# Layer 0 of a two-layer image network: turning a tile by VectorE blocks and DRAM instead of TensorE, adding the bias on TensorE, subtracting maxima on GpSimd

## The chip, the cores and the metric

The kernel runs on one core of a Trainium2 chip. The core has four computing engines that follow their own instruction streams: TensorE (PE; weight loads are shown apart as PEld), VectorE (DVE), ScalarE (ACT) and GpSimd (POOL). SyncE (SP) issues nearly all transfers between DRAM and on-chip memory (SBUF); TensorE's results arrive in PSUM. The metric is the time on the device in microseconds. The kernel before takes 9257.28 us (median of 3 runs, 9252.85 to 9259.84).

## The reference

The input is 8 images of 128x128 points with 128 channels. Two layers follow each other. Layer 0 is a linear attention, and is the only one that the change touches (N = 128x128, NH = 4 heads of HD = 32):

```python
qkv = einsum('bhwc,cf->bhwf', x, w_qkv); q, k, v = split(qkv, 3)
q, k, v = (t.reshape(B, NH, HD, N) for t in (q, k, v))      # a plain reshape of the memory
q = softmax(q, axis=-2) * HD**-0.5
k = softmax(k, axis=-1)
context = einsum('bhdn,bhen->bhde', k, v)
attn = einsum('bhde,bhdn->bhen', context, q).reshape(B, H, W, 128)
out = einsum('bhwf,fc->bhwc', attn, w_out) + b_out
out = (out - mean(out)) * rsqrt(var(out) + 1e-3) * gamma + beta   # over the channels
x = out + x
```

Layer 1 is a selective scan over each image in four directions: a projection to 512 columns, a 3x3 depthwise convolution, the scans, a gate `silu(z)` on their sum, a layer norm and an output projection. Its gate z is a product of layer 0's output, and the kernel computes it at the end of layer 0.

## The kernel before, in words

The program has three stages one after the other: `layer0`, `layer1_front` and `layer1_scan`. The change lies in `layer0` alone.

`layer0` holds two images in SBUF (`xs`), channels in the partitions and points (w, h) along the free side. An image is worked in NG = 32 groups of GW = 4 columns w, 512 points each. `image(b)` runs two things at once: `attend(b)`, which computes the output of image b, and `context(b + 1)`, which computes the context of the next image from its keys and values. Image -1 has only a context, image 7 (the last) only an attention. The plain reshape of the reference makes each image row h one of its 128 rows (head and d) and puts w and channel along n, so the softmax of k runs along w and channels of one h, and a maximum is needed for each of the 128 h before the exponential. `context` keeps it per section of BK = 4 groups and rescales the sum (`total`) when a new section begins.

The stages of `context` for group g: `key` (matmul, copy to SBUF on ACT), `larger` (running maximum of four groups on VectorE; after the fourth it is cut down to 128 columns in two steps, L196 and L197), `fold` (TensorE turns the maximum, VectorE reduces it to a column m, compares it with the earlier one, forms the exponent a of the rescaling and a diagonal matrix dg), `spread` (a matmul of ones with dg puts the maxima along the free side, in the PSUM tile pm), `subtract` (k minus pm, VectorE L231), `raise_to` (exp on ACT), `value` (matmul, copy on ACT) and `add` (four pairs of matmuls into pc, and once per section total on VectorE).

The stages of `attend`: `query` (matmul into pq, maximum qm L270 and subtraction L272 on VectorE), `exponent` (ACT L275), `normalize` (sum L280 and reciprocal L281 on VectorE, product L282 on GpSimd), `through_wo` (matmuls into pg, copy gt on ACT), `through_context` (matmul into po; VectorE adds the bias, L296, which moves the tile to SBUF as o; ACT squares it, L298), `variance` (VectorE sums the squares, L302), `scale` (GpSimd: var, rstd by a power, L310, and a diagonal matrix d of rstd for each column, L313), `turn` (TensorE multiplies o by d, L321: up to here h is in the partitions and w and channel along the free side; this scales the tile and turns it so that channels are in the partitions again) and `finish` (ACT applies gamma and beta, L325; GpSimd adds x, L327; for half of the images the result is stored, L330). The weights `wo` and the bias `bb` have their means taken off beforehand, so out is already centred.

The order of work is written out by hand. `in_order` makes each engine (SP too) run its instructions in the order in which the program emits them. `image` has one loop over t; in step t each stage works on group t minus its own lag, and contexts lag one step more (`later`, a = t - later). So an instruction that waits holds back all that follows on its engine. The list of `at(...)` calls in `image` is this order.

`gate_group` computes the gate z of layer 1: for some images VectorE first copies the group with w and h exchanged (L152), then two matmuls, two Silu on ACT and two stores. `gate(b - 1)` does this for a whole image after step 0 of image b and then loads image b + 1. In the last image the gates of images 6 and 7 are done inside the steps, two groups per step. Silu and exp each make ACT load their table (ACT_TABLE_LOAD) when they alternate.

PSUM tiles of `layer0` share six slots (`ps`), taken in turn.

Of the kernel before, what the change touches and what calls it, by code (L numbers as in the profile page):

```python
# [8 lines left out]
F32 = mybir.dt.float32  # L9
# [23 lines left out]
NCH = L // CH  # L33
EPS0 = 1e-3
EPS1 = 1e-5


NAT, TURN = 0, 1
# [39 lines left out]
def layer0(ctx: ExitStack, tc, xT, w_qkv, w_out, b_out, gamma, beta, win, x1, zs):  # L78
# [15 lines left out]
    sm = ctx.enter_context(tc.tile_pool(name="l0s", bufs=4))  # L94
    ps = ctx.enter_context(tc.tile_pool(name="l0p", bufs=6, space=PSUM))
    psc = ctx.enter_context(tc.tile_pool(name="l0pc", bufs=1, space=PSUM))

    ident = const.tile([P, P], F32, name="ident")
    make_identity(nc, ident)
# [8 lines left out]
    nc.sync.dma_start(wz, win[:, NC2 * P :])  # L108
    wo = const.tile([P, P], F32, name="wo")
    nc.sync.dma_start(wo, w_out)  # L110
    bb = const.tile([P, GW, P], F32, name="bb")
    for i in range(GW):
        nc.sync.dma_start(bb[:, i, :], b_out.to_broadcast([P, P]))
    gb = const.tile([P, 2], F32, name="gb")
    nc.sync.dma_start(gb[:, 0:1], gamma)
    nc.sync.dma_start(gb[:, 1:2], beta)

    mean = const.tile([P, 2], F32, name="mean")
    nc.vector.tensor_reduce(mean[:, 0:1], wo, AX.X, ALU.add)
    nc.vector.tensor_reduce(mean[:, 1:2], bb[:, 0, :], AX.X, ALU.add)  # L120
    nc.vector.tensor_scalar(mean, mean, 1.0 / P, None, ALU.mult)
    nc.vector.tensor_scalar(wo, wo, mean[:, 0:1], None, ALU.subtract)
    nc.vector.tensor_scalar(bb, bb, mean[:, 1:2], None, ALU.subtract)

    xs = [const.tile([P, W, H], F32, name=f"x{i}") for i in range(2)]
    vts, ctxs = [], []
# [46 lines left out]

    def context(b):

        ks, pks, ms, runs, scales = {}, {}, {}, {}, {}

        def key(g):
            pk = ps.tile([P, GW, P], F32, name="pk", tag="ps")
            nc.tensor.matmul(pk, wq[:, P : 2 * P], group(b, g), start=True, stop=True)  # L180
            ks[g] = k = wp.tile([P, GW, P], F32, name="k", tag="k", bufs=7)
            nc.scalar.copy(k, pk)
            pks[g] = pk

        def larger(g):
            pk = pks.pop(g)
            j, i = divmod(g, BK)
            if i == 1:
                runs[j] = run = wp.tile([P, GW, P], F32, name="run")
                nc.vector.tensor_tensor(run, pk, ks[g - 1], ALU.max)  # L190
            elif i > 1:
                nc.vector.tensor_tensor(runs[j], pk, runs[j], ALU.max)

            if i == BK - 1:
                run = runs[j]
                nc.vector.tensor_tensor(run[:, 0:2], run[:, 0:2], run[:, 2:4], ALU.max)  # L196
                nc.vector.tensor_tensor(run[:, 0], run[:, 0], run[:, 1], ALU.max)  # L197

        def fold(g):

            j, i = divmod(g, BK)
            if i < BK - 1:
                return
            run = runs.pop(j)
            turned = ps.tile([P, P], F32, name="pmt", tag="ps")
            nc.tensor.transpose(turned, run[:, 0, :], ident)
            ms[j] = m = sm.tile([P, 1], F32, name="m")
            nc.vector.tensor_reduce(m, turned, AX.X, ALU.max)
            if j:
                nc.vector.tensor_tensor(m, m, ms[j - 1], ALU.max)  # L210
                scales[j] = a = sm.tile([P, 1], F32, name="a")
                nc.vector.tensor_tensor(a, ms.pop(j - 1), m, ALU.subtract)
            runs[j] = dg = sm.tile([P, P], F32, name="dg", bufs=2)
            nc.vector.tensor_scalar(dg, ident, m, None, ALU.mult)

        def spread(g):
            j, i = divmod(g, BK)
            if i == BK - 1:
                nc.tensor.matmul(pm[:, j % 2, :], ones, runs.pop(j), start=True, stop=True)
                if j:  # L220
                    nc.scalar.activation(scales[j], scales[j], AF.Exp)

        def value(g):
            pv = ps.tile([P, GW, P], F32, name="pv", tag="ps")
            nc.tensor.matmul(pv, wq[:, 2 * P : 3 * P], group(b, g), start=True, stop=True)
            nc.scalar.copy(vts[g % 3][:, :, 0:P], pv)

        def subtract(g):

            mb = pm[:, g // BK % 2 : g // BK % 2 + 1, :]  # L230
            nc.vector.tensor_tensor(ks[g], ks[g], mb.to_broadcast([P, GW, P]), ALU.subtract)  # L231
# [26 lines left out]

        return key, larger, fold, spread, value, subtract, raise_to, add

    def attend(b):

        cn = ctxs[b % 2]
        qs, gs, os, vs, ys = {}, {}, {}, {}, {}

        def query(g):
            pq = ps.tile([P, GW * NH, HD], F32, name="pq", tag="ps")
# [22 lines left out]
            nc.scalar.copy(gt, pg)  # L290

        def through_context(g):
            po = ps.tile([P, GW, P], F32, name="po", tag="ps")
            nc.tensor.matmul(po, cn, gs.pop(g), start=True, stop=True)
            os[g] = o = wp.tile([P, GW, P], F32, name="o", bufs=3)
            nc.vector.tensor_tensor(o, po, bb, ALU.add)  # L296
            vs[g] = sq = wp.tile([P, GW, P], F32, name="sq")
            nc.scalar.activation(sq, o, AF.Square)  # L298

        def variance(g):  # L300
            var = sm.tile([P, GW], F32, name="var")
            nc.vector.tensor_reduce(var, vs[g], AX.X, ALU.add)  # L302
            vs[g] = var

        def scale(g):

            var = vs[g]
            nc.gpsimd.tensor_scalar(var, var, 1.0 / P, EPS0, ALU.mult, ALU.add)
            rstd = sm.tile([P, GW, 1], F32, name="rstd")
            nc.gpsimd.tensor_tensor(rstd[:, :, 0], var, half, ALU.pow)  # L310
            vs[g] = d = wp.tile([P, GW, P], F32, name="d")
            i3 = ident.rearrange("p (o c) -> p o c", o=1)
            nc.gpsimd.tensor_tensor(  # L313
                d, i3.to_broadcast([P, GW, P]), rstd.to_broadcast([P, GW, P]), ALU.mult
            )

        def turn(g):
            o, d = os.pop(g), vs.pop(g)
            ys[g] = pt = ps.tile([P, GW, P], F32, name="pt", tag="ps")
            for i in range(GW):  # L320
                nc.tensor.matmul(pt[:, i, :], o[:, i, :], d[:, i, :], start=True, stop=True)  # L321

        def finish(g):
            y = wp.tile([P, GW, P], F32, name="x1t")
            nc.scalar.activation(y, ys.pop(g), AF.Identity, bias=gb[:, 1:2], scale=gb[:, 0:1])  # L325
            xg = group(b, g)
            nc.gpsimd.tensor_tensor(xg, y, xg, ALU.add)  # L327
            if g % 2 == 1 and ORDER[b] >= B // 2:
                t = xs[b % 2][:, (g - 1) * GW : (g + 1) * GW, :].rearrange("p w h -> p (w h)")
                nc.sync.dma_start(x1[ORDER[b]][:, (g - 1) * GN : (g + 1) * GN], t)  # L330

        return query, exponent, normalize, through_wo, through_context, variance, scale, turn, finish

    def image(b):

        key = larger = fold = spread = value = subtract = raise_to = add = None
        query = exponent = normalize = through_wo = through_context = None
        variance = scale = turn = finish = None
        later = LATER if b >= 0 else 0
        if b + 1 < B:  # L340
            key, larger, fold, spread, value, subtract, raise_to, add = context(b + 1)
        if b >= 0:
            (query, exponent, normalize, through_wo, through_context, variance, scale, turn,
             finish) = attend(b)

        def at(stage, g):
# [2 lines left out]

        for t in range(later + NG + BK + 2):  # L350
            a = t - later
            at(scale, t - 2)
            at(finish, t - 3)
            at(query, t)
            if b == B - 1 and t < NG:
                gate_group(b - 1, t)
            at(through_wo, t - 1)
            if b == B - 1 and 4 <= t < NG + 4:
                gate_group(b, t - 4)
            at(exponent, t)  # L360
            at(subtract, a - BK - 1)
            at(raise_to, a - BK - 1)
            at(key, a)
            at(normalize, t)
            at(fold, a - 1)
            at(value, a - BK - 1)
            at(larger, a)
            at(through_context, t - 1)
            at(add, a - BK - 2)
            at(turn, t - 2)  # L370
            at(spread, a - 1)
            at(variance, t - 1)
            if t == 0 and 0 < b < B - 1:
                gate(b - 1)
# [895 lines left out]
```

## Time and profile before

| | |
|---|---|
| median of the runs | 9257.28 us |
| the profiled execution | 9261.02 us |
| its span, first to last instruction | 9259.2 us |
| mean granted TensorE clock | 0.796 |
| busy over the span: PE, DVE, ACT, POOL | 68%, 86%, 77%, 79% |
| layer 0: up to | 2388 us |
| reciprocal of total (a context is complete), L252 | 110.0, 337.0, 634.8, 933.5, 1221.7, 1507.7, 1804.2, 2099.0 us |
| gate of a whole image, image 3 | from about 936 to 997 us |
| DMA, 0 to 2300 us | 112 GB/s mean |

The profile is of one execution. A line of a group gives the line of the kernel, the engine, the operation, output and input names with their shapes, the count, busy time, the mean of one in ns, the idle time of the engine just ahead of these instructions and what ended it. A line of the timeline gives start and duration in us. Idle time that is marked `<-ACT sq` ended when ACT's instruction that wrote sq was done.

### The profile page before, as it was taken

To read this page: it belongs to the slowest core of one execution; us is meant where nothing else is said; L and a number is where in the kernel's file an instruction comes from. 1 tells how busy PE (TensorE), PEld (TensorE's weight loads), DVE (VectorE), ACT (ScalarE), POOL (GpSimd) and SP (SyncE) were. 2 spreads that over 40 slices of the span, in tenths; PEclk is the share of its full clock that TensorE was granted. 3 is DMA by queue.
4 is the path that set the end of the run, shared out by engine and by line. 5 is a ranking of instruction groups with operands and counts; after the bars stand their busy time and mean duration, and the time that the engine had idled before them with its cause. 6 is when DMAs were issued, how large, how long until landed. Compare 5 with 4: busy or idle time off the path is not lost. (4 is left out here: it accounts for less than half of the span.)

```text
span 9259.2 us, 91316 instructions
## 1 busy us (share of the span) xinstructions
PE 6337.5 (68%) x24512; PEld 3096.6 (33%) x24512; DVE 7992.0 (86%) x7953; ACT 7099.7 (77%) x8066; POOL 7316.5 (79%) x4684
## 2 busy tenths in 40 slices
PE   8899998988899999999434636446364463643636
PEld 5555555554333333333101304114031140311403
DVE  6667666774699999999799999999999999999996
ACT  5555555657789999999688887887878888888885
POOL 3446444554588988888599899998999989999897
PEclk9999999999999999999655757557575575755857
DMA  1322333123478789888758769587695876957767
GB/s 76 146 84 96 137 121 146 70 109 137 148 242 249 251 246 244 245 246 241 206 154 238 208 185 258 158 230 216 179 260 159 222 225 178 257 165 218 230 174 211
DMA packets 934769, 1750.66 MB, mean 189 GB/s; under 512 B 150228, under 2 KB 376148, under 8 KB 926064
## 3 DMA queue, kind: packets, MB, share of 16 engines
q1 hardware_dynamic: 873328, 1509.92, 49.4%
q0 software_dynamic: 60928, 234.90, 13.8%
q8 instruction: 200, 3.28, 0.1%
q14 instruction: 313, 2.56, 0.1%
HBM read 1052.36 MB, written 692.12 MB: 188 GB/s over the span
## 5 line engine op out<-in xcount | busy, mean ns | idle before, releaser
L951 POOL TENSOR_TENSOR h<-ubt,sp 128x1024 f32<-128x1024 f32 x1024 | 2422.4, 2399 | 348.4 <-ACT mv L1058 124.1
L934 PE MATMUL px<-rows,dtw 128*128 128x512 bf16 x2048 | 953.5, 565 | 2266.2 <-DVE y L1001 1084.5
L534 DVE SCALAR_TENSOR_TENSOR acc<-xb,cw,acc 128x1024 f32<-128x1024 f32 x1024 | 1320.3, 1289 | 133.7 <-ACT xb L502 89.9
L526 POOL TENSOR_TENSOR tap<-tap 128x1024 f32<-128x1024 f32 x512 | 1224.0, 2394 | 243.9 <-ACT tap L524 220.6
L938 ACT ACTIVATE sp<-px 128x1024 f32<-128x1024 f32 x1024 | 1047.3, 1024 | 435.4 <-PE px L934 418.1
L961 DVE TENSOR_TENSOR_SCAN h<-px,h 128x1024 f32<-128x1024 f32 x512 | 1177.3, 2331 | 31.7 <-ACT px L942 15.1
L934 PEld LDWEIGHTS <-dtw 128*128 128x128 bf16 x2048 | 169.1, 110 | 3089.1 <-issue 1022.7
L959 DVE TENSOR_TENSOR_SCAN h<-px,h 128x1024 f32<-128x1024 f32 x512 | 1177.9, 2330 | 21.4 <-POOL h L951 18.8
L1009 POOL TENSOR_TENSOR y<-y,h 128x512 f32<-128x512 f32 x768 | 1159.8, 1559 | 3.8 <-DVE h L982 3.8
L942 ACT ACTIVATE px<-sp,sa 128x1024 f32<-128x1024 f32 x1024 | 1110.4, 1109 | 6.1
L515 PE MATMUL acc<-xi,wt 128*128 128x512 f32 x2048 | 938.3, 601 | 53.7 <-ACT ures L539 53.7
L524 ACT ACTIVATE tap<-xb,cw 128x1024 f32<-128x1024 f32 x768 | 837.3, 1139 | 15.2 <-POOL xb L499 15.1
L282 POOL TENSOR_TENSOR q<-q,qs 128x512 f32<-128x512 f32 x256 | 272.2, 1063 | 695.5 <-DVE qs L281 695.5
L938 ACT ACT_TABLE_LOAD x512 | 656.9, 1283 | 170.0 <-PE px L934 168.0
L942 ACT ACT_TABLE_LOAD x512 | 656.9, 1283 | 9.1
L1074 PEld LDWEIGHTS px<-wg,z 128*128 128x128 f32 x4096 | 575.3, 225 | 114.8 <-issue 109.1
L1074 PE MATMUL px<-wg,z 128*128 128x128 f32 x4096 | 574.7, 308 | 0.0
L967 PE MATMUL pc<-rows,csel 128*128 128x512 bf16 x1024 | 517.5, 586 | 78.2 <-DVE rstd L1062 74.5
L515 PEld LDWEIGHTS acc<-xi,wt 128*128 128x128 f32 x2048 | 375.1, 189 | 574.4 <-issue 411.9
L488 PE MATMUL pxb<-xi,wi 128*128 128x512 f32 x1024 | 496.2, 607 | 2.1 <-ACT xb L497 2.1
L298 ACT ACTIVATE sq<-o 128x512 f32<-128x512 f32 x256 | 161.2, 630 | 421.0 <-DVE o L296 419.8
L1001 DVE TENSOR_TENSOR y<-y,px 128x1024 f32<-128x1024 f32 x384 | 468.6, 1220 | 14.4
(153 smaller groups left out, 15038.8 us busy)
## 6 DMA issues: line engine op xcount, KB each, us to landing
ubt<-ubs SPq DMA_DIRECT2D x1024, 512.0 KB
zs<-z SPq DMA_DIRECT2D x512, 256.0 KB
ubs<-ures SPq DMA_DIRECT2D x256, 512.0 KB
ubs<-turned SPq DMA_DIRECT2D x256, 512.0 KB
z<-zs SPq DMA_DIRECT2D x256, 512.0 KB
y<-gs POOLq DMA_DIRECT2D x128, 1024.0 KB, 10.3
gs<-du POOLq DMA_DIRECT2D x96, 1024.0 KB, 8.6
rows<-xps SPq DMA_DIRECT2D x1536, 60.0 KB
```

Of the source, the lines that this page charges most:

```text
L515: nc.tensor.matmul(acc[:, s, :], wt[:, j, c, :], x, start=(j == 0), stop=(j == len(ON_PE) - 1))
L524: nc.scalar.activation(t, at(n, c, *d), AF.Copy, scale=weight(n, c, *d))
L526: nc.gpsimd.tensor_tensor(sums[n, c], sums[n, c], t, ALU.add)
L534: nc.vector.scalar_tensor_tensor(acc, at(n, c, *d), weight(n, c, *d), acc, ALU.mult, ALU.add)
L934: nc.tensor.matmul(p[:, hf * 512 : hf * 512 + 512], sl.dw[:, c * P : c * P + P], src, start=True, stop=True)
L938: nc.scalar.activation(t, da[n, c], AF.Softplus)
L942: nc.scalar.activation(da[n, c], sp[n, c], AF.Exp, scale=sa[:, sl.s, c : c + 1])
L951: nc.gpsimd.tensor_tensor(h, u, t, ALU.mult)
L959: nc.vector.tensor_tensor_scan(e[:, ::-1], x[:, ::-1], e[:, ::-1], start, ALU.mult, ALU.add)
L961: nc.vector.tensor_tensor_scan(e, x, e, start, ALU.mult, ALU.add)
L1009: nc.gpsimd.tensor_tensor(v[:, c], v[:, c], h[:, c], ALU.add)
L1074: nc.tensor.matmul(po[:, w, :], z[:, c, w * H : w * H + H], wg[:, c, :], start=(c == 0), stop=(c == NC2 - 1))
```

## The change

The change lies in `layer0`, and nothing changes elsewhere.

The bias is added by TensorE: `bb` is split into three bf16 parts that add up to it, each part is put into one row (partitions 0, 32 and 64) of `brow`, and a matmul with the selector `bsel` adds these rows into po ahead of the context's product. ACT then squares po straight from PSUM. `scale` becomes `deviation` and no longer forms d. `turn` is done by VectorE: it multiplies po by rstd into o, transposes o in blocks of 32x32, and for every second group the blocks of two groups are written to a DRAM tile `swap` by one transfer and read back by four, each of which fills one quadrant of 32 partitions, so that the whole tile is turned. `finish` reads it from SBUF. The key subtraction moves from VectorE to GpSimd; for that `spread` copies the maxima from PSUM to an SBUF tile mb on ACT. The exponent a and the diagonal dg move to GpSimd too. The running maximum is cut down by one reduction. The order of the stages and their lags change: `finish` works on group t - 5 (was t - 3), `spread` on a - 2 (was a - 1), `turn` stands after `exponent`, `subtract` and `raise_to` after `through_context`.

```diff
+BL = 32
+NB = P // BL
...
+    dram = ctx.enter_context(tc.tile_pool(name="l0d", bufs=3, space=DRAM))
...
-    bb = const.tile([P, GW, P], F32, name="bb")
-    for i in range(GW):
-        nc.sync.dma_start(bb[:, i, :], b_out.to_broadcast([P, P]))
+    bb = const.tile([P, P], F32, name="bb")
+    nc.sync.dma_start(bb, b_out.to_broadcast([P, P]))
...
+    parts = const.tile([P, 3, P], BF16, name="bparts")
+    split3(nc.vector, [parts[:, j] for j in range(3)], bb)
+    brow = const.tile([P, 1, P], BF16, name="brow")
+    nc.vector.memset(brow, 0.0)
+    bsel = const.tile([P, P], BF16, name="bsel")
+    nc.vector.memset(bsel, 0.0)
+    for j in range(3):
+        nc.vector.tensor_copy(brow[BL * j : BL * j + 1, 0, :], parts[BL * j : BL * j + 1, j, :])
+        nc.vector.memset(bsel[BL * j : BL * j + 1, :], 1.0)
...
                 run = runs[j]
-                nc.vector.tensor_tensor(run[:, 0:2], run[:, 0:2], run[:, 2:4], ALU.max)
-                nc.vector.tensor_tensor(run[:, 0], run[:, 0], run[:, 1], ALU.max)
+                runs[j] = top = sm.tile([P, P], F32, name="top", bufs=2)
+                nc.vector.tensor_reduce(top, run.rearrange("p w h -> p h w"), AX.X, ALU.max)
...
-                nc.vector.tensor_tensor(a, ms.pop(j - 1), m, ALU.subtract)
+                nc.gpsimd.tensor_tensor(a, ms.pop(j - 1), m, ALU.subtract)
             runs[j] = dg = sm.tile([P, P], F32, name="dg", bufs=2)
-            nc.vector.tensor_scalar(dg, ident, m, None, ALU.mult)
+            nc.gpsimd.tensor_scalar(dg, ident, m, None, ALU.mult)
...
                 nc.tensor.matmul(pm[:, j % 2, :], ones, runs.pop(j), start=True, stop=True)
+                mbs[j] = mb = sm.tile([P, 1, P], F32, name="mb", bufs=2)
+                nc.scalar.copy(mb[:, 0, :], pm[:, j % 2, :])
...
-            mb = pm[:, g // BK % 2 : g // BK % 2 + 1, :]
-            nc.vector.tensor_tensor(ks[g], ks[g], mb.to_broadcast([P, GW, P]), ALU.subtract)
+            mb = mbs[g // BK]
+            nc.gpsimd.tensor_tensor(ks[g], ks[g], mb.to_broadcast([P, GW, P]), ALU.subtract)
...
-            po = ps.tile([P, GW, P], F32, name="po", tag="ps")
-            nc.tensor.matmul(po, cn, gs.pop(g), start=True, stop=True)
-            os[g] = o = wp.tile([P, GW, P], F32, name="o", bufs=3)
-            nc.vector.tensor_tensor(o, po, bb, ALU.add)
+            os[g] = po = ps.tile([P, GW, P], F32, name="po", tag="ps")
+            nc.tensor.matmul(po, bsel, brow.to_broadcast([P, GW, P]), start=True, stop=False)
+            nc.tensor.matmul(po, cn, gs.pop(g), start=False, stop=True)
             vs[g] = sq = wp.tile([P, GW, P], F32, name="sq")
-            nc.scalar.activation(sq, o, AF.Square)
+            nc.scalar.activation(sq, po, AF.Square)
...
-            vs[g] = d = wp.tile([P, GW, P], F32, name="d")
-            i3 = ident.rearrange("p (o c) -> p o c", o=1)
-            nc.gpsimd.tensor_tensor(
-                d, i3.to_broadcast([P, GW, P]), rstd.to_broadcast([P, GW, P]), ALU.mult
-            )
-        def turn(g):
-            o, d = os.pop(g), vs.pop(g)
-            ys[g] = pt = ps.tile([P, GW, P], F32, name="pt", tag="ps")
-            for i in range(GW):
-                nc.tensor.matmul(pt[:, i, :], o[:, i, :], d[:, i, :], start=True, stop=True)
+        def turn(g):
+            o = wp.tile([P, GW, P], F32, name="o", bufs=1)
+            nc.vector.tensor_tensor(o, os.pop(g), vs.pop(g).to_broadcast([P, GW, P]), ALU.mult)
+            if g % 2 == 0:
+                ts[g // 2] = wp.tile([P, NB, 2, P], F32, name="blocks")
+            t = ts[g // 2]
+            nc.vector.transpose(
+                t[:, :, g % 2, :].rearrange("p j (w b) -> p w j b", b=BL),
+                o.rearrange("p w (j a) -> p w j a", a=BL),
+            )
+            if g % 2 == 0:
+                return
+            d = dram.tile([P, NB, 2 * P], F32, name="swap")
+            nc.sync.dma_start(d, ts[g // 2].rearrange("p j g x -> p j (g x)"))
+            ts[g // 2] = u = wp.tile([P, NB, 2, P], F32, name="turned")
+            src = d.rearrange("(i a) j x -> j a i x", a=BL)
+            for j in range(NB):
+                nc.sync.dma_start(u[BL * j : BL * j + BL].rearrange("p i g x -> p i (g x)"), src[j])
 
         def finish(g):
             y = wp.tile([P, GW, P], F32, name="x1t")
-            nc.scalar.activation(y, ys.pop(g), AF.Identity, bias=gb[:, 1:2], scale=gb[:, 0:1])
+            u = ts[g // 2][:, :, g % 2, :].rearrange("p i (w b) -> p w i b", b=BL)
+            nc.scalar.activation(
+                y.rearrange("p w (i b) -> p w i b", b=BL), u, AF.Identity, bias=gb[:, 1:2], scale=gb[:, 0:1]
+            )
...
-            at(scale, t - 2)
-            at(finish, t - 3)
+            at(deviation, t - 2)
+            at(finish, t - 5)
             at(query, t)
...
-            if b == B - 1 and 4 <= t < NG + 4:
-                gate_group(b, t - 4)
+            if b == B - 1 and 5 <= t < NG + 5:
+                gate_group(b, t - 5)
+            at(spread, a - 2)
             at(exponent, t)
-            at(subtract, a - BK - 1)
-            at(raise_to, a - BK - 1)
+            at(turn, t - 2)
             at(key, a)
             at(normalize, t)
             at(fold, a - 1)
             at(value, a - BK - 1)
             at(larger, a)
             at(through_context, t - 1)
+            at(subtract, a - BK - 1)
+            at(raise_to, a - BK - 1)
             at(add, a - BK - 2)
-            at(turn, t - 2)
-            at(spread, a - 1)
             at(variance, t - 1)
```

More of the change, by code (lines that the diff above doesn't have):

```diff
@@ L119, in layer0 @@
     nc.vector.tensor_reduce(mean[:, 0:1], wo, AX.X, ALU.add)
-    nc.vector.tensor_reduce(mean[:, 1:2], bb[:, 0, :], AX.X, ALU.add)
+    nc.vector.tensor_reduce(mean[:, 1:2], bb, AX.X, ALU.add)
     nc.vector.tensor_scalar(mean, mean, 1.0 / P, None, ALU.mult)
@@ L174, in context @@
     def context(b):
-        ks, pks, ms, runs, scales = {}, {}, {}, {}, {}
+        ks, pks, ms, runs, scales, mbs = {}, {}, {}, {}, {}, {}
         def key(g):
@@ L203, in fold @@
                 return
-            run = runs.pop(j)
+            top = runs.pop(j)
             turned = ps.tile([P, P], F32, name="pmt", tag="ps")
-            nc.tensor.transpose(turned, run[:, 0, :], ident)
+            nc.tensor.transpose(turned, top, ident)
             ms[j] = m = sm.tile([P, 1], F32, name="m")
@@ L263, in attend @@
         cn = ctxs[b % 2]
-        qs, gs, os, vs, ys = {}, {}, {}, {}, {}
+        qs, gs, os, vs, ts = {}, {}, {}, {}, {}
         def query(g):
@@ L303, in variance, with deviation @@
             vs[g] = var
-        def scale(g):
+        def deviation(g):
             var = vs[g]
             nc.gpsimd.tensor_scalar(var, var, 1.0 / P, EPS0, ALU.mult, ALU.add)
-            rstd = sm.tile([P, GW, 1], F32, name="rstd")
+            vs[g] = rstd = sm.tile([P, GW, 1], F32, name="rstd")
             nc.gpsimd.tensor_tensor(rstd[:, :, 0], var, half, ALU.pow)
-            vs[g] = d = wp.tile([P, GW, P], F32, name="d")
-            i3 = ident.rearrange("p (o c) -> p o c", o=1)
-            nc.gpsimd.tensor_tensor(
-                d, i3.to_broadcast([P, GW, P]), rstd.to_broadcast([P, GW, P]), ALU.mult
-            )
-        def turn(g):
-            o, d = os.pop(g), vs.pop(g)
-            ys[g] = pt = ps.tile([P, GW, P], F32, name="pt", tag="ps")
-            for i in range(GW):
-                nc.tensor.matmul(pt[:, i, :], o[:, i, :], d[:, i, :], start=True, stop=True)
+        def turn(g):
[7 more added lines that the diff above has]
+                o.rearrange("p w (j a) -> p w j a", a=BL),
+            )
+            if g % 2 == 0:
[6 more added lines that the diff above has]
+                nc.sync.dma_start(u[BL * j : BL * j + BL].rearrange("p i g x -> p i (g x)"), src[j])
         def finish(g):
             y = wp.tile([P, GW, P], F32, name="x1t")
-            nc.scalar.activation(y, ys.pop(g), AF.Identity, bias=gb[:, 1:2], scale=gb[:, 0:1])
+            u = ts[g // 2][:, :, g % 2, :].rearrange("p i (w b) -> p w i b", b=BL)
+            nc.scalar.activation(
+                y.rearrange("p w (i b) -> p w i b", b=BL), u, AF.Identity, bias=gb[:, 1:2], scale=gb[:, 0:1]
+            )
             xg = group(b, g)
@@ L330, in finish @@
                 nc.sync.dma_start(x1[ORDER[b]][:, (g - 1) * GN : (g + 1) * GN], t)
-        return query, exponent, normalize, through_wo, through_context, variance, scale, turn, finish
+        return query, exponent, normalize, through_wo, through_context, variance, deviation, turn, finish
     def image(b):
@@ L337, in image @@
         query = exponent = normalize = through_wo = through_context = None
-        variance = scale = turn = finish = None
+        variance = deviation = turn = finish = None
         later = LATER if b >= 0 else 0
@@ L342, in image @@
         if b >= 0:
-            (query, exponent, normalize, through_wo, through_context, variance, scale, turn,
+            (query, exponent, normalize, through_wo, through_context, variance, deviation, turn,
              finish) = attend(b)
```

## The prediction

> **What bounds the kernel now.** I read the page first, then busy time by stage; only the first of the kernel's three stages is edited. The two lines are layer 0 and the front of layer 1:
>
> ```profile
> 0.00:2388.00 2388.00, 2142.07 (x9408) 1297.39 (x9408) 1537.33 (x2660) 1437.79 (x2438) 1156.51 (x1286) 0.98 0.29 113
> 2388.00:4510.00 2122.00, 1894.28 (x4856) 712.24 (x4856) 1933.13 (x1575) 1867.62 (x2044) 1817.48 (x1083) 0.98 0.83 239
> ```
>
> Columns: window, length, then PE, PEld, DVE, ACT, POOL busy, granted clock, DMA share, GB/s. Layer 0 takes 2388 of 9259.2 us, and since the next stage begins when it ends, what it gains or loses moves the end one for one. PE is its busiest engine. Yet VectorE's instructions in order of time, in the middle of image 3, show what sets the pace:
>
> ```profile
> 1116.13 0.69 DVE L302 TENSOR_REDUCE var<-sq 128x4 f32<-128x512 f32 x1 [0.50 <-ACT sq L298]
> 1116.73 0.68 DVE L270 TENSOR_REDUCE qm<-pq 128x16 f32<-128x512 f32 x1
> 1117.51 0.69 DVE L272 TENSOR_TENSOR q<-pq,qm 128x512 f32<-128x512 f32 x1
> 1118.12 0.68 DVE L231 TENSOR_TENSOR k<-k,pmx 128x512 f32<-128x512 f32 x1
> 1118.90 0.69 DVE L280 TENSOR_REDUCE qs<-q 128x16 f32<-128x512 f32 x1
> 1119.62 0.25 DVE L281 RECIPROCAL qs<-qs 128x16 f32<-128x16 f32 x1
> 1119.97 0.69 DVE L192 TENSOR_TENSOR run<-pk,run 128x512 f32<-128x512 f32 x1
> 1120.57 0.68 DVE L296 TENSOR_TENSOR o<-po,bb 128x512 f32<-128x512 f32 x1
> 1122.01 0.69 DVE L302 TENSOR_REDUCE var<-sq 128x4 f32<-128x512 f32 x1 [0.76 <-ACT sq L298]
> ```
>
> From var to var 5.88 us pass, with one gap of 0.76: o goes to ACT to be squared and comes back. Every fourth step also folds the keys' maxima: the starts of qm at 1103.84, 1110.84, 1116.73, 1122.61 and 1130.01 give steps of 7.00, 5.89, 5.88 and 7.40, 26.17 us for four. The instruction groups between 1025 and 1195 us show what makes the long steps long, and GpSimd's work (busy, mean ns, idle before):
>
> ```profile
> L196 DVE TENSOR_TENSOR run<-run 128x256 f32<-128x256 f32 x6 | 6.9, 1144 | 0.2
> L212 DVE TENSOR_TENSOR a<-m 128x1 f32<-128x1 f32 x6 | 5.8, 969 | 0.2
> L327 POOL TENSOR_TENSOR x<-x1t,x 128x512 f32<-128x512 f32 x26 | 33.1, 1275 | 0.0
> L282 POOL TENSOR_TENSOR q<-q,qs 128x512 f32<-128x512 f32 x26 | 27.3, 1049 | 0.0
> L313 POOL TENSOR_TENSOR d<-ident,rstd 128x512 f32<-128x512 f32 x26 | 27.1, 1041 | 2.0
> L310 POOL TENSOR_TENSOR rstd<-var,half 128x4 f32<-128x4 f32 x26 | 26.5, 1019 | 2.2
> ```
>
> A one-column subtraction (a) takes 0.97 us there. The last image (2100 to 2388) has no keys but two gates per step; its step is 8.75 us, 85% of it ACT. The waits from 2130 to 2370 have this line (total, times, longest), 1.59 us a step:
>
> ```profile
> ACT sq L298 <- DVE o L296: 44.4, 28, 1.6
> ```
>
> [...] L196 takes 1.14 us beside GpSimd's q, 0.42 at 1022.78. [...] 1.275 us where both inputs are full tiles (L327), 1.05 where one is a broadcast column (L282). [...]
>
> **The change, part by part** (durations of the profiled run).
>
> *VectorE, per step.* Gone: bias add o (0.68) and key subtraction (0.68). Added: the multiply by rstd out of PSUM (like L272, 0.69) and the transpose T. [...] Its ends: 0.49 (L123's tensor_scalar over 128x512) [...]. I take 0.72. In the new order the distances between VectorE's starts add up to 0.60+0.78+0.72+0.72+0.64+0.72+0.35+0.61 = 5.14 us (var, qm, q, multiply, T, sum, reciprocal, run), with no round trip through ACT. Every fourth step the strided maximum (0.69) replaces L196 and L197; a and dg leave.
>
> *GpSimd, per step.* Gone: d (1.04). Added: the key subtraction, 1.27 like L327, since mb is a tile too (ends 1.05 and 1.27). In a fold step also a (0.2, like L308's 0.194) and dg (0.3, like the 0.29 of the 128x128 identity). The subtraction now stands inside a loop between two engines: reciprocal, gap 0.15, q 1.01, subtraction 1.23, var 0.28, rstd 1.02, gap 0.06, multiply 0.72, T 0.64, sum 0.72, reciprocal 0.25, together 6.08 us. That exceeds 5.14, so it is the new bound. GpSimd's x (1.27) lies beside multiply to reciprocal (2.33) and is hidden. A fold step adds a and dg, 0.5, and m, [...] 0.3. A spread step adds ACT's copy of mb and exp of a, 0.2 each, before exp q, which has 0.23 of slack: 0.17. Four steps: 4x6.08+0.8+0.17 = 25.3, 0.87 less than 26.17. Seven images have 27 such steps: 0.87x6.75x7 = -41 us.
>
> *Early steps* (the first five of an image, no subtraction yet) fall from 5.65 to VectorE's 5.15: -0.5x5x7 = -17.
>
> *TensorE.* Eight turning matmuls go (0.86 by their starts) and one bf16 matmul comes (an f32 matmul is two passes that advance by 0.43 each and take 0.59; L934's shortest bf16 one takes 0.38, 0.21 less, so about 0.22). Its work falls from 25.0 to some 22.5 us per four steps, hidden under 25.3: worth nothing by itself. po now stays in PSUM until the multiply, where pt stood. The six slots suffice except in the last image, where the fourth gate matmul needs po's slot, free 2.95 us after the square; ACT wants that gate 4.3 after it. Hidden, just.
>
> *Swap through DRAM.* Per two groups one 512 KB write, SP's wait, four 128 KB reads. The last x1 store has the write's size (SP's issue, then who waited):
>
> ```profile
> 2385.11 0.32 SPq L330 DMA_DIRECT2D x<-x  x1
> 2388.18 0.20 POOL masks.py:197 MEMSET ident<- 128x128 f32 x1 [3.09 <-DMA x<-x]
> ```
>
> So 3.1 us. For a read's landing I take 2.2, the time after which a small write (4514.37) let its reader issue (4516.55). Four issues at 0.38 come first: R = 0.1+3.1+0.1+1.5+2.2 = 7.0, 9 with traffic. What covers it: the transpose ends 5.19 after the previous step's reciprocal, and finish on ACT stands 2x6.08+3.0 after it, which leaves 10.0. Upper end: the chain of work that ended last has "DMA out<-r" with 14.00 us. Behind SP's wait stand the stores of x1 and z; x1's issue falls after the reads, and z has seven buffers.
>
> *Image ends.* The last transpose, R and two finishes are not covered by full steps: 12.5 after the last qm, +8, then 6.9 of ACT, PE and total, 27.4 against 26.5 now. I take 2 each: +14. *Start:* three bias DMAs fewer ahead of x, 0.47 each: -1; the bias split hides under x's first load (15.4), and would cost 3 without it.
>
> *Last image.* sq reads PSUM, so its wait of 1.59 goes. But the swap's write stands behind the fourth z store on SP: R is 9.5 to 10 from that gate, and 4.8 from finish to the fourth gate again, some 14.5 for two steps, 7.3 each. I take 7.5 for 8.75: -1.25x31 = -39. Its end adds +6.
>
> Sum: -41-17+14-1-39+6 = **-78 us**, from 9261.0 of the profiled execution (span 9259.2 and 1.8 around it) to 9183. The median shown is 3.7 below that execution: **9180**.
>
> **Rivals.** *Transpose dear (ends slower).* T is 1.25, [...]. 189 full and 35 early steps carry it, so each 0.1 us adds 22: T=1.25 gives 9180+119 = 9300, and it decides from 1.07. For: [...] there is no row. [...]
>
> *The swap is late (slower).* From R about 10 finish holds ACT, in order, ahead of exp q. Then four steps cost R plus the 14.3 from a finish to the next turn but one. R=12: 26.3, +47; early +29; ends +32; last image +25: 9313. It decides near 11. For: rows of 1 KB, the 14.00. Against: DMA share is 0.11 in mid-image.
>
> *Subtraction cheap.* 1.05 makes the loop 5.86, -0.9 per four: 9140.
>
> *Cancelled.* The change doesn't do what it says in the full steps: the loop, in-order ACT and folds take 26.1 as now, and the last image gives half. 9250.
>
> **How the numbers follow.** Forecast 0.50 (own range 9130 to 9225), cheap subtraction 0.10, cancelled 0.10, dear transpose 0.17, late swap 0.13. Faster by over 0.2% (18 us, about what a measurement of this kernel can tell): 0.60; same 0.10; slower 0.30. The range 9120 to 9340 holds the first three and both slow cases up to T=1.4 or R=12.4.
>
> **What would show it.** A transpose row near 0.7 us; qm distances of 6.1 with VectorE idle before the multiply, released by rstd; a fold step of 6.9; no wait of x1t for the DMA of "turned" in mid-image; a last-image step of 7.5 without sq's wait; layer 0 ending near 2310. The prediction is wrong if the transpose passes 1 us, if x1t waits in every second step, or if layer 0 ends where it did.

## The result, and the profile after

The changed kernel takes 9310.53 us (median; 9305.94 to 9312.46), the kernel before beside it 9257.34. The ratio is 1.0056, with a 95% interval of 1.0044 to 1.0069. The change makes the kernel slower, where the prediction had 9180 and faster.

The profiled execution's span is 9310.5 us against 9259.2, 51.3 more. Busy time by stage (columns as in the prediction's first fence) puts 47 of them in layer 0, which now ends at 2435 us:

```profile
0.00:2435.00 2435.00, 2100.55 (x7616) 1086.83 (x7616) 1473.33 (x2489) 1411.12 (x2502) 1262.23 (x1406) 0.95 0.46 166
2435.00:4557.00 2122.00, 1893.32 (x4856) 711.91 (x4856) 1933.54 (x1577) 1870.10 (x2045) 1818.55 (x1084) 0.98 0.83 238
```

The front of layer 1 is unchanged. In layer 0 VectorE has 64 us less to do and GpSimd 106 us more (1156.51 before), and the granted clock is 0.95 instead of 0.98.

The place within layer 0 follows from two kinds of marks in the timeline: the reciprocals that complete a context, and the starts of qm. All figures in us; "early steps" are the five after an image's first step, "full steps" the 25 that follow to the start of its last, an "image end" from the last qm of an image to the first of the next.

| | before | after | difference | predicted |
|---|---|---|---|---|
| start, to the first context complete | 110.0 | 107.4 | -3 | -1 |
| early steps, 7 images | 267.6 | 253.5 | -14 | -17 |
| full steps, 7 images of 25 | 1141.1 | 1092.9 | -48 | -41 |
| image ends, 7 | 7 x 27.23 | 7 x 35.08 | +55 | +14 |
| last context complete at | 2099.02 | 2089.57 | -9 | |
| last image, from there to the end of layer 0 | 289.2 | 345.5 | +56 | -33 |

So the part that the prediction spent most words on came out as it said, and the changed kernel is 9 us ahead when the last image begins. It loses the time at the ends of images and in the last image.

**Full steps.** VectorE's instructions in order of time in the middle of image 3, after, from one var to the next:

```profile
1111.46 0.67 DVE L316 TENSOR_REDUCE var<-sq 128x4 f32<-128x512 f32 x1
1112.22 0.69 DVE L285 TENSOR_REDUCE qm<-pq 128x16 f32<-128x512 f32 x1
1112.95 0.69 DVE L287 TENSOR_TENSOR q<-pq,qm 128x512 f32<-128x512 f32 x1
1114.74 0.69 DVE L328 TENSOR_TENSOR o<-po,rstd 128x512 f32<-128x512 f32 x1 [1.10 <-POOL rstd L324]
1115.47 0.71 DVE L332 STREAM_TRANSPOSE blocks<-o 128x512 f32<-128x512 f32 x1
1116.11 0.65 DVE L295 TENSOR_REDUCE qs<-q 128x16 f32<-128x512 f32 x1
1116.79 0.25 DVE L296 RECIPROCAL qs<-qs 128x16 f32<-128x16 f32 x1
1116.96 0.63 DVE L205 TENSOR_TENSOR run<-pk,run 128x512 f32<-128x512 f32 x1
1117.62 1.04 DVE L210 TENSOR_REDUCE top<-run 128x128 f32<-128x512 f32 x1
1118.58 0.68 DVE L316 TENSOR_REDUCE var<-sq 128x4 f32<-128x512 f32 x1
```

The one gap is ahead of o, and GpSimd's rstd ends it. This is the predicted picture: VectorE waits once a step for the loop that runs through GpSimd. The four steps from 1087.16 to 1112.22 take 6.94, 5.66, 6.52 and 5.94 us, and so it goes on in every four: 25.07 (predicted 25.3, before 26.17). A plain step was predicted at 6.08 and a step with a fold at 6.9. The instruction groups between 1022 and 1192 us, after, give the prices (busy, mean ns of one, then the idle time ahead of them):

```profile
L246 POOL TENSOR_TENSOR k<-k,mb 128x512 f32<-128x512 f32 x27 | 34.3, 1271 | 0.0
L332 DVE STREAM_TRANSPOSE blocks<-o 128x512 f32<-128x512 f32 x27 | 19.2, 712 | 0.9
L328 DVE TENSOR_TENSOR o<-po,rstd 128x512 f32<-128x512 f32 x27 | 18.7, 692 | 26.1 <-POOL rstd L324 26.0
L210 DVE TENSOR_REDUCE top<-run 128x128 f32<-128x512 f32 x7 | 7.3, 1046 | 0.2
L223 DVE TENSOR_TENSOR m<-m 128x1 f32<-128x1 f32 x6 | 6.3, 1053 | 0.2
L227 POOL TENSOR_SCALAR dg<-ident,m 128x128 f32<-128x128 f32 x7 | 4.3, 608 | 0.0
```

Transpose and subtraction cost what was taken for them (0.712 and 1.271; the 0.72 taken for the transpose was the author's estimate). The strided maximum, m and dg cost more (below).

**The last image.** Its step was 8.7 us and is now 9.4 or about 11.1 (mean 10.33). One slow step in the timeline of the last image, after, with the instructions that release one another, and x1t:

```profile
2178.77 0.63 ACT L290 ACTIVATE q<-q 128x512 f32<-128x512 f32 x1
...
2179.78 0.81 ACT L348 ACTIVATE x1t<-turned,gb 128x512 f32<-128x512 f32 x1
...
2180.58 1.05 POOL L297 TENSOR_TENSOR q<-q,qs 128x512 f32<-128x512 f32 x1 [5.84 <-PE pz L174]
...
2181.87 1.02 POOL L324 TENSOR_TENSOR rstd<-var,half 128x4 f32<-128x4 f32 x1
...
2182.86 1.26 POOL L352 TENSOR_TENSOR x<-x1t,x 128x512 f32<-128x512 f32 x1
...
2184.18 3.63 PE L174 MATMUL pz<-x,wz 128*128 128x512 f32 x4 [1.34 <-POOL x L352]
...
2187.89 0.60 ACT L176 ACTIVATE z<-pz 128x512 f32<-128x512 f32 x1 [1.00 <-PE pz L174]
2188.51 1.28 ACT L290 ACT_TABLE_LOAD   x1
...
2189.80 0.63 ACT L290 ACTIVATE q<-q 128x512 f32<-128x512 f32 x1
```

It is a closed loop of 11.03 us: the exponential of q (ACT), its sum and reciprocal (VectorE, not shown), q's product, rstd and x (GpSimd, in order), the gate's matmuls, which wait for x, their Silu, the table load (1.28), and the next exponential. x1t started at 2179.78, long before x, so the transfer through DRAM isn't what is late here. In the kernel before no gate matmul waits for x in this stretch; the gate stands ahead of the x of its step:

```profile
2180.43 1.88 PE L161 MATMUL pz<-x,wz 128*128 128x512 f32 x4
...
2182.57 1.27 POOL L327 TENSOR_TENSOR x<-x1t,x 128x512 f32<-128x512 f32 x1
```

The two lengths of the step go with TensorE's granted clock. Two steps of the changed kernel (columns as before; the clock is the third number from the right):

```profile
2203.08:2212.47 9.39, 7.50 (x23) 3.26 (x21) 4.17 (x9) 7.33 (x11) 3.46 (x5) 1.00 0.44 170
2180.87:2191.90 11.03, 8.44 (x21) 3.82 (x21) 4.17 (x8) 7.14 (x11) 3.46 (x5) 0.85 0.37 143
```

From the sixth step on, every step at a clock of 1.00 takes 9.3 to 9.4 us, every other, at 0.69 to 0.85, 10.7 to 11.5.

**The image ends.** The timeline of an image end, after (end of image 3); SP's write and reads of the swap, then ACT and GpSimd in turn:

```profile
1196.52 0.34 SPq L339 DMA_DIRECT2D swap<-blocks  x1
...
1199.21 1.74 SPq L343 DMA_DIRECT2D turned<-swap  x4
...
1204.02 0.82 ACT L348 ACTIVATE x1t<-turned,gb 128x512 f32<-128x512 f32 x1 [0.46 <-DMA turned<-swap]
...
1204.91 1.27 POOL L352 TENSOR_TENSOR x<-x1t,x 128x512 f32<-128x512 f32 x1 [2.02 <-ACT x1t L348]
...
1206.14 1.26 POOL L246 TENSOR_TENSOR k<-k,mb 128x512 f32<-128x512 f32 x1
1207.43 0.63 ACT L249 ACTIVATE k<-k 128x512 f32<-128x512 f32 x1 [2.12 <-POOL k L246]
1207.97 0.80 ACT L348 ACTIVATE x1t<-turned,gb 128x512 f32<-128x512 f32 x1
...
1208.85 1.27 POOL L352 TENSOR_TENSOR x<-x1t,x 128x512 f32<-128x512 f32 x1 [1.45 <-ACT x1t L348]
```

From the swap's write to the x1t that needs it 7.5 us pass, 2.69 of them up to SP's first read: the predicted 7 to 9. But from one x1t to the next 3.95 us pass, because both engines are in order and hand over twice a step: x1t (ACT), x and then the subtraction (GpSimd), the exponential (ACT), the next x1t. Before, VectorE did the last three of these subtractions in one go:

```profile
1215.25 1.87 DVE L231 TENSOR_TENSOR k<-k,pmx 128x512 f32<-128x512 f32 x3
```

The waits of layer 0, after (total, times, longest):

```profile
ACT k L249 <- POOL k L246: 515.1, 231, 4.1
...
ACT x1t L348 <- DMA turned<-swap: 33.7, 13, 5.9
```

Of the subtraction's 515 us some 103 lie in the seven image ends. Of the swap's 33.7 only 2.6 do; 28.6 are the first `finish` of six images, in the early steps.

### The profile page after: what moved, and what is told of

The parts are those of the page before. It is cut to its first block, busy times and chain, and to the rows that moved or that the text cites. A ratio compares the mean times of both kernels' runs of the same rounds, so it can differ in the third digit from the quotient of the medians.

```text
span 9310.5 us, 87781 instructions
## 1 busy us (share of the span) xinstructions
PE 6293.5 (68%) x22720; PEld 2882.5 (31%) x22720; DVE 7927.0 (85%) x7782; ACT 7079.5 (76%) x8130; POOL 7422.3 (80%) x4804
## 5 line engine op out<-in xcount | busy, mean ns | idle before, releaser
L249 ACT ACTIVATE k<-k 128x512 f32<-128x512 f32 x256 | 161.8, 632 | 515.8 <-POOL k L246 515.1
L176 ACT ACTIVATE z<-pz 128x512 f32<-128x512 f32 x512 | 301.2, 599 | 249.5 <-PE pz L174 194.5
```

## The experiments

The theory after the comparison: the last image is slow because the gate of a group now stands in the same step as its `finish` (group t - 5 for both; before, `finish` worked on t - 3 and the gate on t - 4, one step apart), and the image ends are slow because the key subtraction on GpSimd alternates with x1t and x. The rivals: the way through DRAM is late in both places, or TensorE's lower clock is the cause and not a consequence.

### The gate one step later in the changed kernel

```diff
-            if b == B - 1 and 5 <= t < NG + 5:
-                gate_group(b, t - 5)
+            if b == B - 1 and 6 <= t < NG + 6:
+                gate_group(b, t - 6)
```

> The changed kernel with one number edited: in the last image the gate of a group comes in the step after the group's finish (lag 6), not in the same step (lag 5), as the kernel before had it (finish 3, gate 4). Theory, same step: TensorE stands ahead of the gate until GpSimd has added x, and all behind it waits. Then the last image's step falls from 10.2 us (mean) to about 7.5, some 70 us in all: about 9240 us. Rival, late swap: finish waits for the transfers, so one step more for the gate changes the step by less than 0.5 us: 9295 to 9310. Rival, slower clock: TensorE's matmuls are slow [...], and stay slow: 9280 to 9310.

Measured: 9228.07 us (9222.98 to 9231.05), ratio to before 0.9968, interval 0.9957 to 0.9980. The last image's steps take 7.78 us, each like the next, and layer 0 ends at 2358.7, 76 us earlier; full steps (25.07) and image ends (34.94) stay. In the timeline of the last image of this experiment the gate's matmuls now start without a wait, before the x of their step:

```profile
2194.16 1.88 PE L174 MATMUL pz<-x,wz 128*128 128x512 f32 x4
2194.34 1.28 POOL L352 TENSOR_TENSOR x<-x1t,x 128x512 f32<-128x512 f32 x1
```

So one lag costs 82 us (`finish` was moved by two steps and the gate by one), and turns the sign of the whole change.

### The same distance in the kernel before

```diff
-            if b == B - 1 and 4 <= t < NG + 4:
-                gate_group(b, t - 4)
+            if b == B - 1 and 3 <= t < NG + 3:
+                gate_group(b, t - 3)
```

> The kernel before with the gate moved into the step of the finish (lag 3 for both, was 3 and 4); nothing else. No transfer through DRAM in it. Same step: the last image's step rises from 8.7 to about 10.4 us, since the gate's matmuls wait for var, rstd, d and x on GpSimd: about 9305 us. Late swap: no swap here, so within 10 us of 9257. Slower clock: [...] within 10 us of 9257.

Measured: 9372.49 us (9368.91 to 9377.84), ratio 1.0123, interval 1.0107 to 1.0140. Only the last image moves: its step goes from 8.69 to 12.45 us, its end from 25.6 to 37.7. This kernel has no swap, and its gates wait for x all the same (last image of this experiment):

```profile
2180.51 1.26 POOL L327 TENSOR_TENSOR x<-x1t,x 128x512 f32<-128x512 f32 x1
...
2181.83 1.98 PE L161 MATMUL pz<-x,wz 128*128 128x512 f32 x4 [3.30 <-POOL x L327]
```

The direction is the theory's; the step grew by about twice what was expected. Part of that is in TensorE's matmuls: in a step of 11.27 us the gate's four passes take 1.98 us (2181.83), in the next, of 12.37 us, 3.10 (2193.09); the longer steps take 12.1 to 13.1 us. Where the other 0.9 us of the 11.27 over the expected 10.4 come from is open.

### Finish and gate both one step later in the changed kernel

```diff
-            at(finish, t - 5)
+            at(finish, t - 6)
...
-            if b == B - 1 and 5 <= t < NG + 5:
-                gate_group(b, t - 5)
+            if b == B - 1 and 6 <= t < NG + 6:
+                gate_group(b, t - 6)
```

> The changed kernel with finish and gate both one step later (lag 6 for both), so that the transfers have a step more and the gate is still in the step of the finish. Late swap: the last image's step falls under 9 us, 9270 us or less. Same step: it stays at 10.2; one step more at each image's end adds up to 3 us: 9305 to 9335.

Measured: 9318.81 us (9316.86 to 9321.68), ratio 1.0067, interval 1.0052 to 1.0082. The swap has a whole step more, and nothing gets better: the last image's step is 10.20 us (10.33), the image ends 37.71 (35.08). A late swap is excluded as the cause in the last image. The distance between finish and gate decides, not the distance between transpose and finish.

### The key subtraction back on VectorE

This kernel starts from the one with the later gate.

```diff
-                mbs[j] = mb = sm.tile([P, 1, P], F32, name="mb", bufs=2)
-                nc.scalar.copy(mb[:, 0, :], pm[:, j % 2, :])
...
-            mb = mbs[g // BK]
-            nc.gpsimd.tensor_tensor(ks[g], ks[g], mb.to_broadcast([P, GW, P]), ALU.subtract)
+            mb = pm[:, g // BK % 2 : g // BK % 2 + 1, :]
+            nc.vector.tensor_tensor(ks[g], ks[g], mb.to_broadcast([P, GW, P]), ALU.subtract)
```

> As e1, and the key subtraction back on VectorE out of PSUM (no copy mb). Theory, loop: q, subtraction, var and rstd on GpSimd are one loop with VectorE and set the 6.04 us of a plain step; without the subtraction the loop is 4.8 and VectorE's own work of 5.8 sets it. Plain step 5.8, fold steps with it; and at image ends GpSimd's x and subtraction no longer alternate with ACT's exp and x1t. Together 40 to 65 us under e1. Rival, that TensorE or ACT sets the step: plain step stays at 6.0, within 20 us of e1. Rival, that VectorE was relieved with use: step 6.3 or more, above e1.

Measured: 9134.81 us (9131.56 to 9137.87), ratio 0.9868, interval 0.9853 to 0.9883. It is 93 us below the kernel that it starts from: 52 in the full steps (1091.7 to 1039.9; four steps 23.79), 38 in the image ends (34.94 to 29.52 each), 4 in the early steps. The move of the subtraction, as it was made, costs these 93 us. VectorE's extra 0.68 us a step is less than the waiting that GpSimd's 1.27 us brings. The gain was larger than expected; the image ends, which the estimate had not valued so high, are a good part of it.

### The subtraction on VectorE only at the image ends

Again from the kernel with the later gate; groups 28 to 31 of each of the eight contexts (the condition `b >= 0` holds for all of them, and 32 such subtractions stand in VectorE's trace).

```diff
+            if b >= 0 and g >= NG - BK:
+                mb = pm[:, g // BK % 2 : g // BK % 2 + 1, :]
+                nc.vector.tensor_tensor(ks[g], ks[g], mb.to_broadcast([P, GW, P]), ALU.subtract)
+                return
```

> The gate experiment's kernel with the key subtraction of the last four groups of an image (28 to 31) on VectorE, all others on GpSimd. Alternation theory for the image ends (x1t on ACT, x and subtraction on GpSimd, exp on ACT follow one another, 3.95 us a step): the mean tail falls from 34.9 to 29 to 31 us, four full steps stay at 25.07, time 9185 to 9205 against 9228. Rival, the tail is set by the swap's way through DRAM (write to last read 7.5 us): the tail falls by less than 2 us, time 9215 to 9230.

Measured: 9197.34 us (9182.52 to 9203.91), ratio 0.9923, interval 0.9907 to 0.9940. The image ends fall from 34.94 to 30.47 us, the full steps stay at 25.07 for four. 7 x 4.47 = 31 us, which is the difference of the medians (the kernel before stood at 9264.86 us beside this one and at 9255.38 beside the other; in the traces the last context is complete at 2060.91 us against 2091.19). The alternation is the larger part of what the image ends lost (7.85 each); the rest, about 3, lies near what the prediction gave (2), but was not taken apart.

### The subtraction stays on GpSimd, earlier in the step

From the kernel with the later gate. `subtract` is issued ahead of `finish`, and `deviation` and `finish` stand behind the query and the gates:

```diff
         for t in range(later + NG + BK + 2):
             a = t - later
-            at(deviation, t - 2)
-            at(finish, t - 5)
             at(query, t)
...
             at(spread, a - 2)
+            at(deviation, t - 2)
+            at(subtract, a - BK - 1)
+            at(finish, t - 5)
             at(exponent, t)
...
             at(through_context, t - 1)
-            at(subtract, a - BK - 1)
             at(raise_to, a - BK - 1)
```

> The gate one step later as in the gate experiment (9228), and the order of the stages changed so that GpSimd's key subtraction stands ahead of finish in a step: it then no longer stands between the reciprocal and the variance of a step. Loop theory: the loop reciprocal, q, var, rstd, multiply, transpose, sum loses the subtraction (1.27 us), 6.08 becomes some 4.9, and VectorE's own 5.14 to 5.4 is the bound: plain steps 5.3 to 5.6, four steps 22.5 to 23.5 instead of 25.07, 70 to 115 us in the full steps. In the tails x1t, x, subtraction, exp no longer follow each other in one step: mean tail 29 to 32 instead of 34.9, 20 to 40 us. Together 9080 to 9140. Rival, GpSimd bound by its sum: its work per step (x 1.27, q 1.01, subtraction 1.27, var 0.28, rstd 1.02, and a, dg in every fourth) is about 4.9 and doesn't bind alone, but if x now delays q's product by its length then four steps stay at 24.5 to 25.5 and the time at 9200 to 9240.

Measured: 9141.23 us (9136.18 to 9145.90), ratio 0.9868, interval 0.9853 to 0.9883. Four full steps take 22.40 us, an image end 29.98. In the middle of image 3 of this experiment GpSimd's subtraction starts when rstd is done, and VectorE's multiply runs beside it:

```profile
1060.26 1.02 POOL L324 TENSOR_TENSOR rstd<-var,half 128x4 f32<-128x4 f32 x1
...
1061.25 1.27 POOL L246 TENSOR_TENSOR k<-k,mb 128x512 f32<-128x512 f32 x1
...
1061.66 0.68 DVE L328 TENSOR_TENSOR o<-po,rstd 128x512 f32<-128x512 f32 x1
...
1064.27 1.05 POOL L297 TENSOR_TENSOR q<-q,qs 128x512 f32<-128x512 f32 x1 [0.35 <-DVE qs L296]
```

VectorE's wait for rstd, 26.0 us in 27 multiplies of the changed kernel, is nearly gone (960 to 1108 us of this experiment):

```profile
L328 DVE TENSOR_TENSOR o<-po,rstd 128x512 f32<-128x512 f32 x27 | 18.6, 689 | 5.0 <-POOL rstd L324 3.9
```

The loop of the prediction loses one member, nothing is taken off any engine, and four steps fall by 2.67 us. Together with the experiment that put the subtraction back on VectorE, this shows the loop; how much of the 2.67 us comes from the new places of `deviation` and `finish`, which moved too, was not measured. The last image pays for the new order: `finish` now stands close ahead of the next step's gate, and its step is 9.36 us in the mean instead of 7.78 (8.43 in five steps from 2123.93 us on, about 10.1 in those around them). This was not expected.

### The same, with the last image's finish ahead of the gates, and a variant for the image ends

```diff
+            if b == B - 1:
+                at(finish, t - 5)
             at(query, t)
...
-            at(finish, t - 5)
+            if b < B - 1:
+                at(finish, t - 5)
```

> The early-subtraction kernel (9141), in which finish stands behind the gates of its step; here the last image alone has finish ahead of the gates again, as in the gate experiment. Theory of the distance between finish and the gate that needs it (the last image's price is set by how much of a step lies between GpSimd's x and the gate's matmul): its steps fall from 9.36 to 7.78 us as in that experiment, its end from 44 to about 34, all else stays (four full steps 22.40, mean tail 30.0): 9141 - 49 - 10 = 9082, between 9070 and 9095. Rival, the last image's steps are long because TensorE's clock falls [...]: they stay above 8.5, 9115 to 9141.

Measured: 9086.89 us (9082.04 to 9094.02), ratio 0.9818, interval 0.9804 to 0.9833. The last image's steps are 7.78 us again, its end 36.4 us; the rest stays (22.40, 29.99). Once more the distance between `finish` and the gate moves the last image. This is the fastest kernel of the study: 1.8% below before.

The variant issues the last three `finish` of an image behind `add` and `variance` of their step, so that ACT need not wait for the swap ahead of the exponentials:

```diff
-            if b < B - 1:
+            if b < B - 1 and t < NG + 2:
                 at(finish, t - 5)
...
             at(variance, t - 1)
+            if b < B - 1 and t >= NG + 2:
+                at(finish, t - 5)
```

> The last image's order restored as in the kernel beside it, and in the image ends (the last three finishes of the first seven images) finish stands behind the exponential and the sums of its step. If the way through DRAM holds the image ends by ACT waiting in order for the turned tile ahead of the exponentials, the mean tail falls from 30.0 to 26 to 28.5 us, 10 to 28 us in all: 9055 to 9075. If only GpSimd's subtractions and the fold set the ends, it stays at 29 to 30.5: 9075 to 9095.

Measured: 9125.33 us (9113.75 to 9126.98), ratio 0.9860, interval 0.9844 to 0.9876. Both expectations fell: the image ends grew, from 29.99 to 33.93. The timeline of an image end of this experiment shows the alternation, with no wait for the swap in these lines:

```profile
1136.08 1.26 POOL L246 TENSOR_TENSOR k<-k,mb 128x512 f32<-128x512 f32 x1
...
1137.38 0.63 ACT L249 ACTIVATE k<-k 128x512 f32<-128x512 f32 x1 [2.13 <-POOL k L246]
1137.91 0.80 ACT L348 ACTIVATE x1t<-turned,gb 128x512 f32<-128x512 f32 x1
...
1138.79 1.26 POOL L352 TENSOR_TENSOR x<-x1t,x 128x512 f32<-128x512 f32 x1 [1.44 <-ACT x1t L348]
1140.01 1.26 POOL L246 TENSOR_TENSOR k<-k,mb 128x512 f32<-128x512 f32 x1
```

1140.01 - 1136.08 = 3.93 us, the same period as in the changed kernel. With `finish` behind the exponential, x1t waits for it, x for x1t, and the next subtraction, in order on GpSimd, for x. What was meant to take ACT's wait away rebuilt the loop that the earlier subtraction had opened.

## Why the prediction was wrong

Point by point, by its own steps.

- **The full steps** (-41) were right: -48. The loop through GpSimd was named with its members, and the experiment that takes the subtraction out of it, with GpSimd still doing it, gains 2.67 us per four steps. Some prices were off: the strided maximum takes 1.05 us (0.69 was taken), dg 0.61 (0.3), m 1.05 (its former 0.51 and 0.3 were taken). That the sum still came out, a little low, is in part luck: two of the four steps are shorter than the plain 6.08 (5.66 and 5.94).
- **The early steps** (-17) and the start (-1) were right: -14 and -3.
- **The swap** is hidden in full steps, as predicted, with R = 7.5 us. The rival of a late swap, like that of a dear transpose, did not happen, though the time came out where these two had put it (9313 and 9300). A time that agrees with a rival is no proof of it: the rows of the profile excluded both.
- **The image ends** (+14) were mis-sized: +55. R and two finishes were counted; that a step of the image end has little else to do, and so falls to the period of the ACT-GpSimd alternation, was not. The term "6.9 of ACT, PE and total" behind the two finishes held no hand-over of these steps to GpSimd, to which the subtraction had moved. The former end was also a little longer (27.2 us in the mean) than the 26.5 it was set against.
- **The last image** (-39, its end +6) holds the step that failed: +56, 89 us off. What failed is the path that was taken to set its pace, from `finish` to the fourth gate and through the swap, 14.5 us for two steps. The path that set it closes within one step: the gate's matmuls wait for x, which GpSimd adds behind q and rstd, and the Silu, the table load and the next exponential follow them, 9.39 us at a clock of 1.00 and 11.03 in the step shown, at 0.85. The prediction took sq's wait away and then asked only when the swap's data arrive. It did not set the lags of `finish` and of the gate side by side: t - 3 and t - 4 before, t - 5 and t - 5 after. With the gate one step later the step measures 7.78 us, near the predicted 7.5, without sq's wait, and the last image takes 267.6 us, 22 less than before, where 33 less were predicted. (The prediction's "85% of it ACT" is a misreading: from 2130 to 2370 us TensorE was busy for 85% and ACT for 81%.)

The two misses, 41 and 89 us, account for the 130 us between 9180 and 9310; the small errors of the other terms, and 4 us outside layer 0, nearly cancel. Seen from the other side: in the kernel as changed, the gate's distance costs 82 us and the subtraction on GpSimd 93, while what remains of the change (the tile turned by VectorE and the swap, the bias on TensorE, the folds on GpSimd, the new order) gains about 120, since the kernel with the other two undone runs at 9134.81 beside 9255.38.

The clock rival fell as a cause of its own: the lower clock goes away (0.99) when the gate is moved by one step and nothing else is changed, so it is a consequence of the order of work. It does add to the loss: in the slow steps the gate's four passes that wait for x take 3.3 to 3.8 us, in those at a clock of 1.00 1.98. Of the 2.55 us between the mean step of 10.33 and 7.78, 1.6 remain at a clock of 1.00 (9.39) and 0.9 come with the lower one.

## What to carry to other kernels

When stages are given new lags, list for every pair of producer and consumer the steps between them before and after; a pair that falls into one step turns a hidden latency into a loop of all engines in between. An operation moved to a less busy engine is priced by the loop that it joins and not by that engine's load, and its place in the order can matter as much as the engine: issuing the subtraction earlier on GpSimd took off 87 us, moving it back to VectorE 93. Price the short steps at the ends of loops by themselves, since there, as here, hand-overs between in-order engines can set the pace.

## What the runs showed of the hardware

- TensorE's granted clock was lower in the last image of the changed kernel, where from 2100 to 2340 us none of TensorE's waits is longer than 1.34 us. The busy times of 2140 to 2340 us, changed kernel (columns as above):

```profile
2140.00:2340.00 200.00, 153.02 (x410) 71.47 (x411) 81.85 (x137) 138.38 (x195) 68.79 (x80) 0.88 0.49 177
```

  and the same stretch with the gate one step later:

```profile
2140.00:2340.00 200.00, 166.09 (x530) 81.26 (x528) 104.84 (x176) 180.40 (x254) 87.98 (x101) 0.99 0.65 236
```

  The gate's four passes at 2184.18 take 3.63 us in a step at a mean clock of 0.85, those at 2206.39 1.98 in a step at 1.00. What lowers the clock was not shown.
- The comparison m, one column, takes 1.05 us on VectorE beside GpSimd's product q and 0.16 in an image end (1196.70), where GpSimd is idle. In a full step the two end together: q runs from 1123.24 for 1.05 us, m from 1123.25 for 1.05. The prediction's 0.3 for m was the author's estimate; why the two end together was not shown.
- Reducing 128x512 to 128x128 over a strided view takes VectorE 1.05 us, a reduction of 512 columns in order, to 16 or 4, 0.64 to 0.69. Whether the stride or the number of results makes the difference was not tried.
- Turning 128x512 f32 in 32x32 blocks takes VectorE 0.712 us, hardly more than the multiply of this size (0.692).
